# Attention scores on tiles of 32 by 64, an earlier weight fetch and six unused products, in a two-layer attention kernel

## The chip, the cores and the metric

The kernel runs on one core of a Trainium2 chip. A core has five engines that work side by side: TensorE (matrix products, PE in the profile, with PEld for its weight loads), VectorE (DVE), ScalarE (ACT), GpSimd (POOL) and SyncE (SP), which here only issues transfers. The metric is the device time of one execution in microseconds (us); lower is better. Runs of the same kernel are compared by their medians.

## The reference: what is computed

The input is a batch of 8 images of 32 by 32 positions with 512 channels. Two layers follow each other; each adds an attention over its group-normalised input to the input. All numbers are float32.

```python
# layer 0: 16 heads of 32 channels
qkv = gn(x) @ w_qkv
attn = softmax(einsum('bhid,bhjd->bhij', q * 32 ** -0.5, k))
x = x + einsum('bhij,bhjd->bhid', attn, v).reshape(B, N, C) @ w_proj + b_proj
# layer 1: 4 heads of 128 channels, with relative positions
q, k, v = gn(x) @ Wq * 128 ** -0.5, gn(x) @ Wk, gn(x) @ Wv
attn = softmax(q @ k.T + relative_logits(q, pos_emb_w, pos_emb_h))
x = x + (attn @ v) @ Wo
```

N is 1024 positions and C is 512 channels. The group norm gn uses 32 groups of 16 channels per image. The change concerns the scores of layer 0, `q @ k` with a depth of only 32 per head, and the first microseconds of the program.

## The kernel before

The batch is walked one image at a time, and the work of neighbouring images is woven together. While layer 0's attention of image b runs (`attention_0`), the projections, the norms and layer 1's attention of the image before it and the projections of the image after it are issued between its steps. A generator yields after each piece, and `side_by_side` draws pieces of the other work in proportion to a cost. Which instruction stands where on each engine is then decided by the framework's scheduler, which keeps the order of the program only where data demand it.

Each projection (`project_T`, `project_rows`, through `seven`) is a product of 512 by 512 with 1024 positions, done with seven block products in place of eight, on sums and differences of weight quarters and of input quarters. `Matrix.add_up` makes the weight sums: it fetches the weights into a block of SBUF (line 137), makes four differences (L142), and stores them to DRAM (L144), from where the stream of weights (`Stream`) takes them later. `forms` (L328 to L331) makes the sums of the normalised input on VectorE. `by_columns` (the matmul of line 308) cuts each product into four of 32 output columns, tiles of 128 rows by 32 columns of the array.

A step of `attention_0` handles four heads at once, for 128 keys and 512 queries. `front` computes the scores: four products, one for each head, each 32 rows deep and 128 columns wide, into the four banks of one PSUM tile `ps` (L525). ScalarE turns them into exponentials (L533), four banks in one instruction. `back` multiplies the exponentials by v: four products of 128 rows by 32 columns into `acc` (L544), while VectorE adds the exponentials up (L553 and L555). `back` of a step is issued after `front` of the next one. There is one `ps` tile, so a `front` waits until the exponential of the step before has read it. There are 4 x 2 x 8 steps for an image, 512 in all. `finish` divides by the sums (L491 to L513).

The start (`load_first`): eight transfers bring the 1024 rows of the first image, four from SP's queue and four from ScalarE's (L717). TensorE transposes them (L729), ScalarE and VectorE copy the results out (L737, L739), VectorE takes statistics (L244, L245), SP stores the transposed rows away (`put_away`, L213), `group_norm` makes mean and variance (L256 to L281), GpSimd the inverse root (L285), and VectorE normalises in place (L288). Then `forms`, and `before_first`, which projects v, q and k. In the program text v's weights are fetched after `load_first`, from ScalarE's queue, and added up on GpSimd; q's and k's are fetched from SP's queue and added up on VectorE. SP's queue also brings the next image's rows in pieces `xs` (L231).

The fetch, as it was:

```python
        def add_up(self, engine, queue, store, keep=False):
            t = block(f"prep_{self.name}")
...
            queue.dma_start(whole, self.w)
```

Of the kernel before, what the change touches and what calls it, by code (L numbers as in the profile page):

```python
# [9 lines left out]
F32 = mybir.dt.float32  # L10
# [7 lines left out]
P = 128  # L18
# [9 lines left out]
def quick_path(  # L28
# [23 lines left out]
    nc = tc.nc  # L52
# [3 lines left out]
    CC = C // P  # L56
    NT = N // P
    NB = 512
    NH = N // NB
    D0 = 32  # L60
    H1, D1 = 4, 128
    HB = P // D0
# [7 lines left out]
    psum = ctx.enter_context(tc.tile_pool(name="psum", bufs=1, space=PSUM))  # L70
# [4 lines left out]
    def block(name, shape=None, dtype=F32):  # L75
        return mem.tile(shape or [P, CC, N], dtype, tag="block", name=name, bufs=BLOCKS)

    def chunks(block):
        return [block[:, i, :] for i in range(CC)]
# [5 lines left out]
    ident = consts.tile([P, P], F32, tag="ident", name="ident")  # L85
# [34 lines left out]
    def quarter(w, i):  # L120
        k, n = i // 10 - 1, i % 10 - 1
        return w[:, k * HC : (k + 1) * HC, n * HN : (n + 1) * HN]

    class Matrix:
# [4 lines left out]
            self.name = name  # L129
            self.w = w.rearrange("(cc p) n -> p cc n", p=P)[:, :, col0 : col0 + NB]  # L130

        def add_up(self, engine, queue, store, keep=False):

            t = block(f"prep_{self.name}")
            whole = t[:, : CC // 2, :].rearrange("p a (b n) -> p (a b) n", n=NB)
            sums = t[:, CC // 2 :, :].rearrange("p a (b c n) -> p (a b) c n", c=HC, n=HN)
            queue.dma_start(whole, self.w)
            b11, b12, b21, b22 = [quarter(whole, i) for i in (11, 12, 21, 22)]
            for i, (x, y) in enumerate(
                [(b12, b11), (b22, sums[:, 0]), (b22, b12), (b21, sums[:, 1])]  # L140
            ):
                engine.tensor_tensor(sums[:, i], x, y, op=ALU.subtract)  # L142
            d = dram.tile([P, 4, HC, HN], F32, tag="sums", name=f"ws_{self.name}", bufs=8)
            store.dma_start(d, sums)  # L144
            self.t = d
            self.kept = (whole, sums) if keep else None
# [70 lines left out]
    def fetch(kept, x):  # L217
        xT = chunks(x)
        for cc in range(CC):
            nc.sync.dma_start(xT[cc], kept[cc])  # L220
        return xT
# [263 lines left out]
    def normalise(dst, acc_sums, name):  # L485

        su = mem.tile([P, NB], F32, tag="rec", name=f"su_{name}", bufs=2)  # L490
        nc.scalar.copy(su, acc_sums)  # L491
        turned = mem.tile([P, NB], F32, tag="rec", name=f"tu_{name}", bufs=2)
        nc.vector.transpose(turned, su)  # L493
        few = turned.rearrange("p (t c) -> p t c", c=32)[:, :, 0]
        rec = mem.tile([P, NB // 32], F32, tag="few", name=f"rc_{name}", bufs=2)
        nc.vector.reciprocal(rec, few)
        at = check_at[0]
        check_at[0] += 1
        nc.vector.tensor_tensor_reduce(
            out=few,  # L500
            in0=few,
            in1=rec,
            op0=ALU.add,
            op1=ALU.max,
            scale=1.0,
            scalar=0.0,
            accum_out=checks[:, at : at + 1],
        )
        nc.vector.transpose(  # L509
            su.rearrange("p (t c) -> p t c", c=32),  # L510
            rec.unsqueeze(2).to_broadcast([P, NB // 32, 32]),
        )
        nc.gpsimd.tensor_tensor(dst, dst, su, op=ALU.mult)  # L513

    def attention_0(q, k, v, b):

        steps = [(m, h, j) for m in (0, 2, 1, 3) for h in range(NH) for j in range(NT)]
        state = {}

        def front(m, h, j):  # L520
            name = f"0_{b}_{m}_{h}_{j}"
            ps = psum.tile([P, HB, NB], F32, tag="ps", name=f"ps_{name}", bufs=1)
            for r in range(HB):
                rows = slice(r * D0, (r + 1) * D0)
                nc.tensor.matmul(  # L525
                    ps[:, r, :],
                    k[m][rows, j * P : (j + 1) * P],
                    q[m][rows, h * NB : (h + 1) * NB],
                    start=True,
                    stop=True,  # L530
                )
            e = mem.tile([P, HB, NB], F32, tag="e0", name=f"e_{name}", bufs=2)
            nc.scalar.activation(e, ps, AF.Exp, scale=D0 ** -0.5)  # L533
            return e

        def back(m, h, j, e):
            name = f"0_{b}_{m}_{h}_{j}"
            if j == 0:
                state["acc"] = psum.tile([P, NB], F32, tag="acc", name=f"acc_{name}", bufs=1)
                state["first"] = e  # L540
            acc = state["acc"]
            for r in range(HB):
                c0 = (m * HB + r) * D0
                nc.tensor.matmul(  # L544
                    acc[r * D0 : (r + 1) * D0, :],
                    v[:, j, c0 : c0 + D0],
                    e[:, r, :],
                    start=(j == 0),
                    stop=(j == NT - 1),
                )  # L550
            if j == 1:
                state["esum"] = mem.tile([P, HB, NB], F32, tag="es0", name=f"es_{name}", bufs=1)
                nc.vector.tensor_add(state["esum"], state["first"], e)  # L553
            elif j > 1:
                nc.vector.tensor_add(state["esum"], state["esum"], e)  # L555
            if j < NT - 1:
                return
            nc.scalar.copy(q[m][:, h * NB : (h + 1) * NB], acc)
            state["ended"] = (m, h, state["esum"])

        def finish(m, h, esum):
            name = f"0_{b}_{m}_{h}"
            su = psum.tile([P, NB], F32, tag="acc", name=f"sums_{name}", bufs=1)
            for r in range(HB):
                nc.tensor.matmul(  # L565
                    su[r * D0 : (r + 1) * D0, :],
                    ones[:, :D0],
                    esum[:, r, :],
                    start=True,
                    stop=True,  # L570
                )
            normalise(q[m][:, h * NB : (h + 1) * NB], su, name)

        pending = None
        for at in steps:
            if "ended" in state:
                finish(*state.pop("ended"))
            e = front(*at)
            if pending is not None:
                back(*pending)  # L580
            pending = (*at, e)
            yield 2
        back(*pending)
        yield 1
        finish(*state.pop("ended"))
# [126 lines left out]
    def load_first(st):  # L712

        rows = block("x_rows", [P, NT, C])
        for t in range(NT):
            queue = nc.scalar if t % 2 else nc.sync
            queue.dma_start(rows[:, t, :], xf[0, t * P : (t + 1) * P, :])  # L717
        x = block("x0T_0")
        xT = chunks(x)
        for h in range(NH):  # L720
            if h == 0:
                whole = psum.tile([P, CC, NB], F32, tag="ps", name="turned_0", bufs=1)
                banks = [whole[:, cc, :] for cc in range(CC)]
            else:
                banks = [bank(f"turned_1_{cc}") for cc in range(CC - 1)]
                banks.append(psum.tile([P, NB], F32, tag="acc", name="turned_1", bufs=1))
            for t in range(NT // NH):
                for cc in range(CC):
                    nc.tensor.transpose(  # L729
                        banks[cc][:, t * P : (t + 1) * P],  # L730
                        rows[:, h * (NT // NH) + t, cc * P : (cc + 1) * P],
                        ident,
                    )
            for cc in range(CC):
                part = xT[cc][:, h * NB : (h + 1) * NB]
                if h == 0 or cc % 2:
                    nc.scalar.copy(part, banks[cc])  # L737
                else:
                    nc.vector.tensor_copy(part, banks[cc])  # L739
        for cc in (1, 0, 3, 2):  # L740
            statistics(st, xT, cc, "0_0")
        st["kept"] = put_away(xT, "0_0")
        run(group_norm(st, xT, "0_0"))
        st["xn"] = forms(x, "xn0_0")
# [139 lines left out]
    WQ0, WK0, WV0 = [Matrix(w_qkv, i * C, f"qkv{i}") for i in range(3)]  # L884
# [17 lines left out]

    states = [{} for _ in range(B)]
    load_first(states[0])
    WV0.add_up(nc.gpsimd, nc.scalar, nc.gpsimd, keep=True)
    for m in (WQ0, WK0):
        m.add_up(nc.vector, nc.sync, nc.gpsimd, keep=True)
    fill_sel()
    stream = Stream(plan)

    def other_sums():
        for m in (WP, WQ1, WK1, WV1, WO):
            m.add_up(nc.gpsimd, nc.gpsimd, nc.gpsimd)
            yield 0

    def at_once(do):
# [538 lines left out]
```

## Time and profile before

| | |
|---|---|
| median of 6 runs | 3912.12 us (3906.47 to 3914.68) |
| the profiled execution | 3911.84 us |
| its span, first to last instruction | 3910.0 us |
| mean granted TensorE clock | 0.994 |
| TensorE busy | 3817.0 us, 98% |
| VectorE busy | 2519.7 us, 64% |
| ScalarE busy | 1724.6 us, 44% |
| GpSimd busy | 620.8 us, 16% |
| first products of the first projection | from 24.34 us |
| first scores of layer 0 | from 77.7 us |
| last scores of layer 0 | at 3455 us |

In the profile's groups a row gives the line, the engine, the operation, what is written from what, the shape and the number of instructions; then the busy time in us and the mean duration in ns; then the idle time of the engine just before these instructions, and what ended it. For TensorE the shape begins with the tile of the array: 32*128 is 32 rows by 128 columns. The ends of matmuls are modelled, so starts say more than durations. A row of the timeline gives start and duration in us, and merges equal neighbours: "x4" is four instructions. A row of the waits names who waited, for whom, the total in us, the number of times and the longest. PEclk is the share of the full TensorE clock that was granted. A float32 product shows as two weight loads and two matmul records, one for each of its two passes.

### The profile page before, as it was taken

What the parts mean: (1) busy time and instruction counts of PE and PEld (TensorE: products, weight loads), DVE (VectorE), ACT (ScalarE), POOL (GpSimd) and SP (SyncE); (2) the same over time, 40 slices, a digit from 0 to 9 for tenths busy, and PEclk for the clock granted to TensorE, in tenths of its full rate; (3) what the DMA queues carried; (4) which work ended last, traced back from release to release, by engine and by line L of the source; (5) the groups of instructions that cost most, each with busy time, mean ns of one, the idle gap of its engine ahead of it and who ended that gap; (6) DMA issues with size and microseconds to landing.
All of it is one profiled execution on the core that took longest, in us unless ns stands there. A gap on an engine that the chain in (4) does not pass through costs nothing. (4 is left out here: it accounts for less than half of the span.)

```text
span 3910.0 us, 71616 instructions
## 1 busy us (share of the span) xinstructions
PE 3817.0 (98%) x30370; PEld 1416.3 (36%) x30370; DVE 2519.7 (64%) x2905; ACT 1724.6 (44%) x1767; POOL 620.8 (16%) x400
## 2 busy tenths in 40 slices
PE   7999899999999999999999999999999999999998
PEld 4222244232443234432343323433234332344353
DVE  5777675576745867468664686656865568754544
ACT  2554453445434454344544445344453445543132
POOL 1341001121101211012111121111200112011101
PEclk9999999999999999999999999999999999999999
DMA  5221120133202322023120241103311122110401
GB/s 172 75 103 57 34 63 1 39 119 69 58 5 66 103 56 55 12 91 86 42 54 17 91 94 39 44 24 97 88 44 31 31 92 68 32 63 18 124 17 23
DMA packets 482951, 234.19 MB, mean 60 GB/s; under 512 B 269600, under 2 KB 461376, under 8 KB 481600
## 3 DMA queue, kind: packets, MB, share of 16 engines
q1 hardware_dynamic: 470464, 212.69, 20.1%
q0 software_dynamic: 2608, 13.70, 0.9%
q8 instruction: 241, 3.95, 0.4%
q10 hardware_dynamic: 9552, 3.15, 0.4%
q14 instruction: 86, 0.70, 0.1%
HBM read 170.72 MB, written 58.72 MB: 59 GB/s over the span
## 5 line engine op out<-in xcount | busy, mean ns | idle before, releaser
L533 ACT ACTIVATE e<-ps 128x2048 f32<-128x2048 f32 x512 | 961.8, 1879 | 845.8 <-PE ps L525 650.1
L555 DVE TENSOR_TENSOR es<-es,e 128x2048 f32<-128x2048 f32 x384 | 888.1, 2313 | 406.0 <-ACT e L533 403.8
L525 PE MATMUL ps<-q,k 32*128 32x512 f32 x4096 | 591.6, 643 | 33.6 <-ACT e L533 33.5
L643 ACT ACTIVATE e<-ps 128x512 f32<-128x512 f32 x512 | 305.7, 597 | 586.2 <-PE ps L641 549.7
L544 PE MATMUL acc<-e,v 128*32 128x512 f32 x4096 | 549.3, 608 | 0.4 <-ACT su L491 0.4
L640 PE MATMUL ps<-q,k 128*128 128x512 f32 x1024 | 523.6, 593 | 0.3 <-DVE posT L626 0.3
L652 PE MATMUL acc<-e,v 128*128 128x512 f32 x1024 | 521.9, 592 | 0.0
L513 POOL TENSOR_TENSOR q<-q,su 128x512 f32<-128x512 f32 x128 | 214.3, 1674 | 1568.0 <-DVE su L509 1567.3
L663 DVE TENSOR_TENSOR es<-es,e 128x512 f32<-128x512 f32 x384 | 291.8, 760 | 264.5 <-ACT e L643 263.2
L641 PE MATMUL ps<-posT,sel 128*128 128x512 f32 x512 | 406.6, 794 | 0.0
L525 PEld LDWEIGHTS ps<-q,k 32*128 32x128 f32 x4096 | 161.7, 183 | 429.6 <-ACT e L533 213.2
L640 PEld LDWEIGHTS ps<-q,k 128*128 128x128 f32 x1024 | 193.6, 190 | 246.1 <-issue 240.6
L652 PEld LDWEIGHTS acc<-e,v 128*128 128x128 f32 x1024 | 193.1, 189 | 146.7 <-issue 105.0
L544 PEld LDWEIGHTS acc<-e,v 128*32 128x32 f32 x4096 | 81.6, 108 | 387.0 <-issue 342.5
L553 DVE TENSOR_TENSOR es<-e,e 128x2048 f32<-128x2048 f32 x64 | 175.1, 2736 | 38.6 <-ACT e L533 38.6
L493 DVE STREAM_TRANSPOSE tu<-su 128x512 f32<-128x512 f32 x128 | 90.6, 708 | 135.8 <-ACT su L491 135.6
L641 PEld LDWEIGHTS ps<-posT,sel 128*128 128x128 f32 x512 | 97.3, 190 | 122.5 <-issue 122.5
L491 ACT COPY su<-sums 128x512 f32<-128x512 f32 x128 | 74.9, 585 | 149.5 <-PE sums L565 81.3
L661 DVE TENSOR_TENSOR es<-e,e 128x512 f32<-128x512 f32 x64 | 44.2, 691 | 145.7 <-ACT e L643 145.7
L626 DVE TENSOR_TENSOR posT<-pp,posT 32x512 fp32r<-32x512 f32 x128 | 111.9, 874 | 32.0 <-ACT posT L621 30.6
L417 POOL TENSOR_TENSOR k<-b_k,p_k 128x512 f32<-128x512 f32 x32 | 50.3, 1570 | 477.8 <-ACT p_k L382 477.8
L621 ACT CAST posT<-pp 32x512 fp32r<-32x512 f32 x128 | 105.8, 827 | 44.8 <-PE pp L608 43.7
(193 smaller groups left out, 4517.4 us busy)
## 6 DMA issues: line engine op xcount, KB each, us to landing
w_qkv<-ws_qkv SPq DMA_DIRECT2D x168, 128.0 KB, 2.5
d<-x0T SPq DMA_DIRECT2D x32, 512.0 KB, 3.4
x1T<-d SPq DMA_DIRECT2D x32, 512.0 KB, 5.1
d<-x1T SPq DMA_DIRECT2D x32, 512.0 KB, 3.6
x2T<-d SPq DMA_DIRECT2D x32, 512.0 KB, 6.2
w_qkv<-in_L_conv_w_qkv SPq DMA_DIRECT2D x126, 128.0 KB, 2.2
out<-ot SPq DMA_DIRECT2D x240, 64.0 KB, 2.0
xs<-in_x SPq DMA_DIRECT2D x224, 64.0 KB, 2.4
```

What stands on the lines that cost most here:

```text
L513: nc.gpsimd.tensor_tensor(dst, dst, su, op=ALU.mult)
L525: nc.tensor.matmul(ps[:, r, :], k[m][rows, j * P : (j + 1) * P], q[m][rows, h * NB : (h + 1) * NB], start=True, stop=True,)
L533: nc.scalar.activation(e, ps, AF.Exp, scale=D0 ** -0.5)
L544: nc.tensor.matmul(acc[r * D0 : (r + 1) * D0, :], v[:, j, c0 : c0 + D0], e[:, r, :], start=(j == 0), stop=(j == NT - 1),)
L553: nc.vector.tensor_add(state["esum"], state["first"], e)
L555: nc.vector.tensor_add(state["esum"], state["esum"], e)
L626: nc.vector.tensor_sub(rest, logits, greater)
L640: nc.tensor.matmul(ps, k[h][:, keys], q[:, h, queries], start=True, stop=False)
L641: nc.tensor.matmul(ps, sel_flat[:, keys], posT[:, h, queries], start=False, stop=True)
L643: nc.scalar.activation(e, ps, AF.Exp, scale=1.0 / math.sqrt(D1))
L652: nc.tensor.matmul(acc, v[:, j, h * D1 : (h + 1) * D1], e, start=(j == 0), stop=(j == NT - 1),)
L663: nc.vector.tensor_add(state["esum"], state["esum"], e)
```

## The change

Three things change.

1. `front` issues eight score products in a step in place of four: for each half of the 128 keys, one for each head, 32 rows by 64 columns. The halves write the lower and the upper 64 partitions of the same four banks.
2. The fetch of weights is taken out of `add_up` into a method of its own. v's weights are fetched in `load_first`, on SP's queue, right behind the rows of the first image; before, they were fetched after `load_first` on ScalarE's queue. The other weights keep their queue and are fetched right ahead of their sums, as before. The block for v's weights is thereby allotted ahead of that of the transposed rows.
3. After the transposes and the copies of `load_first`, six products of the identity with the first six rows tiles (128 by 128, 512 columns) are issued into a PSUM tile of their own that nobody reads.

```diff
+        def fetch(self, queue):
+            t = self.t = block(f"prep_{self.name}")
+            whole = t[:, : CC // 2, :].rearrange("p a (b n) -> p (a b) n", n=NB)
+            queue.dma_start(whole, self.w)
+
+        def add_up(self, engine, store, keep=False):
+
+            t = self.t
...
-        def add_up(self, engine, queue, store, keep=False):
-
-            t = block(f"prep_{self.name}")
...
-            queue.dma_start(whole, self.w)
...
         def front(m, h, j):
             ps = psum.tile([P, HB, NB], F32, tag="ps", name=f"ps_{name}", bufs=1)
-            for r in range(HB):
-                rows = slice(r * D0, (r + 1) * D0)
-                nc.tensor.matmul(
-                    ps[:, r, :],
-                    k[m][rows, j * P : (j + 1) * P],
-                    q[m][rows, h * NB : (h + 1) * NB],
-                    start=True,
-                    stop=True,
-                )
+            for i in range(2):
+
+                some = slice(64 * i, 64 * i + 64)
+                for r in range(HB):
+                    rows = slice(r * D0, (r + 1) * D0)
+                    nc.tensor.matmul(
+                        ps[some, r, :],
+                        k[m][rows, j * P + 64 * i : j * P + 64 * i + 64],
+                        q[m][rows, h * NB : (h + 1) * NB],
+                        start=True,
+                        stop=True,
+                    )
...
             queue.dma_start(rows[:, t, :], xf[0, t * P : (t + 1) * P, :])
+        WV0.fetch(nc.sync)
         x = block("x0T_0")
...
+        idle = psum.tile([P, CC, NB], F32, tag="ps", name="idle", bufs=1)
+        for t in range(6):
+            nc.tensor.matmul(idle[:, t % CC, :], ident, rows[:, t, :], start=True, stop=True)
         for cc in (1, 0, 3, 2):
             statistics(st, xT, cc, "0_0")
...
-    WV0.add_up(nc.gpsimd, nc.scalar, nc.gpsimd, keep=True)
+    WV0.add_up(nc.gpsimd, nc.gpsimd, keep=True)
     for m in (WQ0, WK0):
-        m.add_up(nc.vector, nc.sync, nc.gpsimd, keep=True)
+        m.fetch(nc.sync)
+        m.add_up(nc.vector, nc.gpsimd, keep=True)
```

More of the change, by code (lines that the diff above doesn't have):

```diff
@@ L912, in other_sums @@
         for m in (WP, WQ1, WK1, WV1, WO):
-            m.add_up(nc.gpsimd, nc.gpsimd, nc.gpsimd)
+            m.fetch(nc.gpsimd)
+            m.add_up(nc.gpsimd, nc.gpsimd)
             yield 0
```

## The prediction

> **What bounds the kernel now.** I read the engine totals first, then the waits of the five middle batches, then the groups, then one score step in the timeline, then the first 31 us.
>
> ```profile
> span 3910.0 us, 71616 instructions
> PE 3817.0 (98%) x30370; PEld 1416.3 (36%) x30370; DVE 2519.7 (64%) x2905; ACT 1724.6 (44%) x1767; POOL 620.8 (16%) x400
> ```
>
> TensorE is busy nearly throughout, the next engine two thirds. Busy matmul time contains fill and drain, so it does not yet say that a nanosecond off TensorE is a nanosecond off the end. The waits from 560 to 3100 us do:
>
> ```profile
> PE y_wo L308 <- DVE a_wo L368: 6.8, 5, 1.4
> PE ps L525 <- ACT e L533: 4.1, 5, 1.1
> PE sums L565 <- ACT q L558: 1.4, 5, 0.3
> ```
>
> That is 12.3 us of waiting in 2540. TensorE's own sequence sets the pace there; over the whole run the scores wait 33.5 us for ScalarE's exponentials, in 28 places near both ends. The groups concerned:
>
> ```profile
> L525 PE MATMUL ps<-q,k 32*128 32x512 f32 x4096 | 591.6, 643 | 33.6 <-ACT e L533 33.5
> L544 PE MATMUL acc<-e,v 128*32 128x512 f32 x4096 | 549.3, 608 | 0.4 <-ACT su L491 0.4
> ```
>
> 4096 records are 512 score steps of four products, each float32 product recorded as two passes. L544 does the same number of 512-column passes in less time, so a score step carries something extra. One step, at 1003.57 to 1005.9 us:
>
> ```profile
> 1003.57 0.40 PE L308 MATMUL z_v<-w_v,x1T 128*32 128x256 f32 x4
> 1003.89 0.71 PE L525 MATMUL ps<-q,k 32*128 32x512 f32 x4
> ...
> 1004.43 0.61 PE L525 MATMUL ps<-q,k 32*128 32x512 f32 x4
> 1004.97 0.64 PE L544 MATMUL acc<-e,v 128*32 128x512 f32 x4
> ```
>
> Read the starts, not the durations. The records' starts (in ns, over all 512 steps, nearly without scatter) give: 429 ns from pass to pass inside one kind of tile; 533 from first to second pass of a score step; 517 from the start of its last product to the first of L544; 453 between L544's two passes; 523 from the last projection product to the score step. Products that run together start 6.7 ns apart. So against 427 ns of streaming, each change of tile form costs 90 to 96 ns, and the first pass after it also shows its weight load: 106 ns for 128 columns, 26 for 32. A step from its first weight load to L544's is 533 + 20 (the fourth product starts 20 ns after the first) + 517 = 1070 ns.
>
> **What the Trainium skill says.** "TensorE: Matmul & The Clock Gate", LDWEIGHTS: a load takes its number of columns divided by 1.2, in ns, whatever the rows: 107 for 128, 53 for 64, 27 for 32. The trace agrees at both ends (106, 26); 64 is not shown. The same page, Part 3, The mechanism: products on different tiles overlap and start about 4 ns apart, matmuls in strict order. Here the spacing is 6.7, and at 99.42 us a product that stands later in the program (z_q, first column tile) starts before three earlier ones (y_q, the other tiles), so the order is not strict across tiles. "TensorEngine Tiling (Array Packing)", Key Properties: changing the tiling mode drains the array; 90 to 96 ns here, and after 128-by-128 tiles it is the same as after 128-by-32, so the columns don't matter. The first page's Part 1 has windows of about 3.4 us after which the clock halves or recovers; here it halves at 14.5 us, 3.6 after the last transpose, and recovers at 28.2.
>
> **The scores, part by part.** Built, the changed kernel has TensorE's order unchanged in all later work; only L525's four products become eight (32 rows by 64 columns, two column halves by four row groups). Per step:
> - Drain before: unchanged, 96, since it belongs to the form that is left. Drain after: unchanged, 90.
> - First-pass load: 64 columns instead of 128. The loads of four row groups run side by side now (106 ns is one load, not four), and so do those of four column tiles in L544 (26 is one of 32 columns, not four). I take it that eight do: 53 exposed, the pass pitch 480. Gain 53. If the halves load one after the other, it stays 106, gain 0.
> - Issue: the eighth product starts 7 × 6.7 = 47 ns after the first, not 20. The drain after a step is counted from its last product (the wait before a step is 523 from the last one, whether 1, 2, 3 or 4 tiles ran before), so this is paid: 27. With the page's 4 ns, an estimate, it would be 16; if the second pass hides it, 0.
> - Streaming: eight 32-by-64 tiles stream the same 2 × 427 ns if all run together. Not shown here; the parts are (four row groups, four column groups).
>
> New step: 480 + 47 + 517 = 1044 against 1070: 26.7 ns less, × 512 = 13.7 us. In the middle nothing covers it, because TensorE waits for nothing. At the ends, where a step waits for the exponential, the chain is step, exponential, step, so the shorter step counts there too. ScalarE and VectorE follow 27 ns earlier per step; with 44% and 64% busy they don't bind.
>
> **The start.** The first projection:
>
> ```profile
> 18.67 2.48 POOL L142 TENSOR_TENSOR prep_qkv<-prep_qkv 128x512 f32<-128x512 f32 x2 [0.87 <-DMA prep_qkv<-in_L_conv_w_qkv]
> 21.24 1.04 POOL L285 TENSOR_TENSOR rstd<-var,neg_half 128x4 f32<-128x4 f32 x1
> 22.27 2.93 POOL L142 TENSOR_TENSOR prep_qkv<-prep_qkv 128x512 f32<-128x512 f32 x2
> ```
> ```profile
> 18.69 1.27 DVE L259 TENSOR_SCALAR avg<-total 128x32 f32<-128x32 f32 x1
> ...
> 20.28 0.89 DVE L281 SCALAR_TENSOR_TENSOR var<-back 128x4 f32<-128x4 f32 x1
> 22.32 4.99 DVE L288 TENSOR_SCALAR x0T<-x0T,back,rstd 128x1024 f32<-128x1024 f32 x4 [1.16 <-POOL rstd L285]
> 27.34 1.23 DVE L328 TENSOR_TENSOR f_xn<-x0T 128x1024 f32<-128x1024 f32 x1
> 28.61 1.22 DVE L329 TENSOR_TENSOR f_xn<-f_xn,x0T 128x1024 f32<-128x1024 f32 x1
> ```
>
> y_v starts at 29.98, when L329 ends, and TensorE then runs nearly full until the first scores at 77.7. So what counts is L329.
> - v's fetch goes from ScalarE's queue (10.9) to SP's behind the rows, where it can issue at 4.38, in the place of the xs loads. Those and SP's later issues move back by about 0.4 us each; nobody needs the xs before 70. Rows and v share the engines at 400 GB/s: rows end near 9, v near 11.3 instead of 18.6.
> - GpSimd's four sums (1.25 each) then run from 11.3 to about 16.5 and leave the norm alone. It slows by their company now: L259 1.27 instead of 0.18, L281 0.89 instead of 0.16, L288 4.99 instead of 2.8 (0.7 each at 394 us). Gain 4.0.
> - The order in the built kernel has a price: q's fetch now stands before the put_away stores, and VectorE's sums of q and k are spread through the norm: six of eight stand before L329, 6 × 0.61 = 3.7 later. The first waits for q's data: 11.3 + 1.3 for three xs (0.2 MB at 150 GB/s) + 2.6 = 15.2, where VectorE arrives at 14.6: 0.6. Queued behind that wait is the whole norm. Bounds 0 to 3.
> - Given back: eight more x_v products done before y_v (four passes of 0.216, 0.9), and a_v, late at 36.84 behind eight sums, no longer late (0.5).
> - The six unused products: 12 passes of 0.43 = 5.1 us from 10.9 to 16, in TensorE's empty time (next work 24.3): nothing, or up to 1 if they ran at half clock. They hold the clock until about 20, not until 24, so I expect it halved again for the first projection. If it held, 8 passes would save 1.7, but y_v waits for L329 anyway: 0 taken, 1.7 at most. The rows' buffer is held 5 us longer; its next user comes after 70.
>
> Sum: −4.0 + 3.7 + 0.6 − 1.4 = −1.1, bounds −4 and +4.
>
> **Sum.** Profiled execution 3911.84 (span 3910.0 and 1.84 around it): −13.7 −1.1 = 3897.0; it lies 0.28 under the median of 3912.12, so 3897.3, given as 3897.
>
> **Rivals.**
> - Issue hidden: the later starts vanish under the first pass. 3912.1 −27.3 −1.1 = 3884. For it: loads do overlap. Against: starts keep their spacing through both passes.
> - Nothing gained: issue is paid in both passes (−53 + 27 + 27), or the start loses what a smaller gain brings. About 3911. Against: today's 20 ns is paid once.
> - Slower: the eight tiles don't run together, at L525's second column half. If its loads wait for the first half's, the pitch stays 533 and only the 27 ns are added: +13.7 −1.1 = 3925. It decides from an exposed load of 80 ns on. The hard form is that the second four products wait until the first four have done both passes, because TensorE does not look far enough ahead: + 853 × 512 = 437 us, 4348. Eight products need 14 later entries set aside, four need 6; only the latter is seen. For both: no 32-by-64 product is in the trace. Against: both directions overlap singly.
>
> **How the numbers follow.** Forecast 0.61, hidden 0.15, nothing gained 0.10, slower by loads 0.09, slower by order 0.05. Forecast and hidden, with the start's bounds, span 3880 to 3902; I carry the range to 3911, so that most of the third case is in and no more than 2 in 10 is out. About 0.2%, 8 us, is what a measurement of this kernel can tell from no change: faster 0.76, within 0.10, slower 0.14.
>
> **What would show it.** L525 as 8192 records of 32*64; pass pitch 480; L544 1044 ns after the step's first load; waits in the middle as small as now. A pitch of 533 shows the serial loads, one near 900 the missing overlap, L544 at 1017 the hidden issue. At the start: y_v near 30, v's sums on GpSimd from 11, the first VectorE sum waiting under 1 us for q, PEclk 0.5 at 24. The forecast is wrong if 64-column loads are not half as long, or if drains depend on columns after all.

## The result, and the profile after

| | before | changed |
|---|---|---|
| median | 3912.48 us (3906.47 to 3915.95, 40 runs) | 3902.11 us (3898.56 to 3907.16, 20 runs) |
| ratio | | 0.9975, 95% interval 0.9969 to 0.9981 |
| the profiled execution, its span | 3911.84 us, 3910.0 us | 3900.62 us, 3898.7 us |
| first score | 77.72 us | 79.26 us |
| first score to the end | 3832.3 us | 3819.5 us |

The change gains 9.8 us by the ratio (7.4 to 12.1). The forecast was 3897; the time is 5 us above it. The page of the changed kernel, answering to the first lines shown of before (busy time, share, instructions):

```profile
span 3898.7 us, 79833 instructions
...
PE 3805.4 (98%) x34478; PEld 1371.1 (35%) x34478; DVE 2516.4 (65%) x2905; ACT 1724.0 (44%) x1767; POOL 622.5 (16%) x400
```

TensorE has 4108 matmuls more, 4096 of them scores and 12 of the unused products, and is busy for 11.6 us less. The groups of the scores and of the products with v:

```profile
L532 PE MATMUL ps<-q,k 32*64 32x512 f32 x8192 | 577.5, 615 | 36.6 <-ACT e L540 36.5
L551 PE MATMUL acc<-e,v 128*32 128x512 f32 x4096 | 547.1, 606 | 0.4 <-ACT su L495 0.4
```

The form is now 32*64 and the count is doubled. One step of the timeline, near the one shown of before:

```profile
994.86 0.39 PE L312 MATMUL z_v<-w_v,x1T 128*32 128x256 f32 x2
995.18 1.11 PE L532 MATMUL ps<-q,k 32*64 32x512 f32 x16
996.22 1.07 PE L551 MATMUL acc<-e,v 128*32 128x512 f32 x8
```

From the scores' first start to that of L551 it is 1.04 us here; before it was 4.97 less 3.89, 1.08. Over all steps the records' starts give 480 ns from the first pass to the second, 47 from a pass's first product to its last, and 517 from the last to L551; from the last product of 512 columns ahead of a step to the step it is 522, as before. The stretch from a step's first product to the next other one, summed over the 64 steps of an image, went from 68.53 to 66.84 us, 26.5 ns a step: 13.5 us in 512 steps.

But from one image to the next the middle went only from 474.5 to 473.2 us (means of five images), 1.3 less where the steps alone give 1.69. What lies beside the steps grew from 406.0 to 406.4 us an image. The waits of TensorE from 560 to 3100 us (total us, times, longest) show where:

```profile
PE y_wo L312 <- DVE a_wo L372: 7.1, 5, 1.4
PE ps L532 <- ACT e L540: 5.2, 5, 1.3
PE sums L572 <- ACT q L565: 1.5, 5, 0.3
```

They were 6.8, 4.1 and 1.4: the three places are the same, and all three have grown, by 1.5 us in five images or 0.3 an image. Where in an image that is, a comparison of ScalarE's exponentials tells: from the 13th of an image to the 21st the time should have fallen by 8 x 26.5 ns, but it was 42.12 us in the kernel before and is 42.19 in the changed one. That is 0.3 of the 0.4 us; the other 0.1 is lost in later steps of the image, where the views list no wait, and stays unexplained. The next lines give the busy time of the engines in that stretch, and for the kernel before also in the 375 us behind it. Before, then changed:

```profile
core 0: us, PE busy (x) PEld busy (x) DVE busy (x) ACT busy (x) POOL busy (x), PEclk, DMA share, GB/s
...
1339.27:1381.39 42.12, 39.98 (x348) 10.67 (x347) 39.60 (x42) 18.22 (x14) 9.09 (x5) 1.00 0.46 84
1381.39:1756.00 374.61, 374.34 (x2952) 148.00 (x2948) 224.94 (x267) 169.75 (x186) 45.25 (x28) 1.00 0.19 52
```
```profile
1335.10:1377.29 42.19, 39.80 (x412) 10.04 (x408) 39.74 (x42) 18.21 (x14) 9.09 (x5) 1.00 0.46 83
```

In the 375 us VectorE is busy for 60% and TensorE waits for nothing. In the 42 us, in which the last projection of one image, the second norm of the next and the exponentials meet, VectorE is busy for 94%, as much as TensorE. Inside the stretch, in the changed kernel:

```profile
1335.10 1.88 ACT L540 ACTIVATE e<-ps 128x2048 f32<-128x2048 f32 x1 [0.44 <-PE ps L532]
1335.89 1.02 POOL L289 TENSOR_TENSOR rstd<-var,neg_half 128x4 f32<-128x4 f32 x1 [1.55 <-DVE var L285]
...
1336.94 2.98 DVE L292 TENSOR_SCALAR x1T<-x1T,back,rstd 128x1024 f32<-128x1024 f32 x4 [1.20 <-POOL rstd L289]
...
1339.84 2.28 DVE L562 TENSOR_TENSOR es<-es,e 128x2048 f32<-128x2048 f32 x1
...
1342.21 1.88 ACT L540 ACTIVATE e<-ps 128x2048 f32<-128x2048 f32 x1 [5.24 <-DVE es L562]
...
1344.15 0.69 PE L532 MATMUL ps<-q,k 32*64 32x512 f32 x8 [0.97 <-ACT e L540]
```

Read it from the bottom: the scores wait for an exponential, that one for a sum on VectorE that is to free a buffer of exponentials, and the sum stands behind the norm's multiplications, which waited for GpSimd's rstd.

The start, first GpSimd, then VectorE:

```profile
13.27 3.72 POOL L146 TENSOR_TENSOR prep_qkv<-prep_qkv 128x512 f32<-128x512 f32 x3 [8.82 <-DMA prep_qkv<-in_L_conv_w_qkv]
...
17.07 1.26 POOL L146 TENSOR_TENSOR prep_qkv<-prep_qkv 128x512 f32<-128x512 f32 x1
```
```profile
17.21 1.67 DVE L146 TENSOR_TENSOR prep_qkv<-prep_qkv 128x512 f32<-128x512 f32 x1 [1.89 <-DMA prep_qkv<-in_L_conv_w_qkv]
...
23.50 0.18 DVE L263 TENSOR_SCALAR avg<-total 128x32 f32<-128x32 f32 x1
...
24.89 0.16 DVE L285 SCALAR_TENSOR_TENSOR var<-back 128x4 f32<-128x4 f32 x1
26.21 2.98 DVE L292 TENSOR_SCALAR x0T<-x0T,back,rstd 128x1024 f32<-128x1024 f32 x4 [1.16 <-POOL rstd L289]
...
31.45 1.21 DVE L333 TENSOR_TENSOR f_xn<-f_xn,x0T 128x1024 f32<-128x1024 f32 x1
```

v's sums end at 18.3 and not at 25.2, and the norm's operations have their short durations: 0.18, 0.16 and 2.98 where they had 1.27, 0.89 and 4.99. But the norm ends no earlier, since six sums for q and k stand in it and the first one waits 1.89 us for its data. Counted from the start of the last transpose of the rows (10.59 us before, 11.44 after; below called "behind the transposes"), y_v starts after 21.37 us (19.39 before), and the first score comes after 67.81 us (67.13 before).

### The profile page after: what moved, and what is told of

Its sections match the earlier page's. It is cut to its first block, busy times and chain, and to the rows that moved or that the text cites. A ratio compares the mean times of both kernels' runs of the same rounds, so it can differ in the third digit from the quotient of the medians.

```text
span 3898.7 us, 79833 instructions
## 1 busy us (share of the span) xinstructions
PE 3805.4 (98%) x34478; PEld 1371.1 (35%) x34478; DVE 2516.4 (65%) x2905; ACT 1724.0 (44%) x1767; POOL 622.5 (16%) x400
## 4 chain that ended last, share of the span: by engine, by line
PE 84%; DVE 9%; ACT 3%; issue 2%; POOL 1%; DMA 1%; SPq 0%; DVEq 0%; POOLq 0%; ACTq 0%
PE ps L647 11%; PE acc L659 11%; PE ps L532 11%; PE acc L551 10%; PE y_k L312 4%; PE y_q L312 4%; PE y_v L312 4%; PE ps L648 3%; PE z_k L312 3%; PE x_v L312 3%; PE x_k L312 3%; PE x_q L312 3%; PE z_v L312 3%; PE z_q L312 2%; ACT e L540 2%; DVE es L562 2%
## 5 line engine op out<-in xcount | busy, mean ns | idle before, releaser
L532 PE MATMUL ps<-q,k 32*64 32x512 f32 x8192 | 577.5, 615 | 36.6 <-ACT e L540 36.5
L551 PE MATMUL acc<-e,v 128*32 128x512 f32 x4096 | 547.1, 606 | 0.4 <-ACT su L495 0.4
L532 PEld LDWEIGHTS ps<-q,k 32*64 32x64 f32 x8192 | 120.4, 130 | 432.6 <-ACT e L540 217.2
L551 PEld LDWEIGHTS acc<-e,v 128*32 128x32 f32 x4096 | 81.5, 108 | 413.6 <-issue 366.0
L633 DVE TENSOR_TENSOR posT<-pp,posT 32x512 fp32r<-32x512 f32 x128 | 111.9, 874 | 31.9 <-ACT posT L628 30.6
```

Of the source, the lines that this page charges most:

```text
L532: nc.tensor.matmul(ps[some, r, :], k[m][rows, j * P + 64 * i : j * P + 64 * i + 64], q[m][rows, h * NB : (h + 1) * NB], start=True, stop=True,
L551: nc.tensor.matmul(acc[r * D0 : (r + 1) * D0, :], v[:, j, c0 : c0 + D0], e[:, r, :], start=(j == 0), stop=(j == NT - 1),)
```

## The experiments

Each was timed beside the kernel before, whose median was 3913.12 us beside e1 to e4, 3911.73 beside e5 to e8 and 3913.91 beside e9 to e12; kernels of different groups are best compared by their ratios.

| kernel | median us | runs | ratio to before, 95% interval |
|---|---|---|---|
| e1, scores alone | 3904.57 | 10 | 0.9976 (0.9967 to 0.9986) |
| e2, early fetch alone | 3913.68 | 13 | 1.0001 (0.9993 to 1.0009) |
| e3, unused products alone | 3910.79 | 13 | 0.9993 (0.9985 to 1.0001) |
| e4, scores on 32 by 32 | 3920.03 | 21 | 1.0020 (1.0013 to 1.0027) |
| e5, changed without unused products | 3901.33 | 7 | 0.9973 (0.9962 to 0.9984) |
| e6, changed, q and k sums after the forms | 3898.39 | 5 | 0.9965 (0.9952 to 0.9979) |
| e7, before, second norm on ScalarE | 3956.60 | 4 | 1.0113 (1.0098 to 1.0129) |
| e8, e1 with the same | 3945.93 | 4 | 1.0093 (1.0078 to 1.0108) |
| e9, before, exponential sum ahead of the norm | 3903.69 | 8 | 0.9972 (0.9961 to 0.9982) |
| e10, e1 with the same | 3890.59 | 5 | 0.9943 (0.9929 to 0.9956) |
| e11, e6 with the same | 3891.22 | 5 | 0.9941 (0.9927 to 0.9954) |
| e12, e11 without unused products | 3889.29 | 5 | 0.9934 (0.9921 to 0.9948) |

### The three parts, each alone (e1, e2, e3)

e1 is the kernel before with the eight products of the diff in `front`. e2 has only the split of the fetch and `WV0.fetch(nc.sync)` behind the rows. e3 has only the six unused products:

```diff
+        idle = psum.tile([P, CC, NB], F32, tag="ps", name="idle", bufs=1)
+        for t in range(6):
+            nc.tensor.matmul(idle[:, t % CC, :], ident, rows[:, t, :], start=True, stop=True)
```

> The kernel before with the eight score products of 32 by 64 alone; the start is as before. Theory A (scores gain in full, the start gives back): a step from its first weight load to the product with v is 480 + 47 + 517 = 1044 ns instead of 1070, times 512 = 13.7 us less, so about 3898.8 us, and the first scores at 77.7 as before. Theory B (part of the scores' gain is lost in waits that grow, and the start is neutral): about 3902, like the whole change.

> The kernel before with the fetch of v's weights behind the first rows and nothing else: four products per score step, no unused products. The order on VectorE becomes that of the changed kernel, with sums of q's and k's weights inside the norm. Theory A: this alone costs 1.6 to 2.7 us, about 3914.5, with the first scores near 79.3 and the first sum on VectorE waiting near 1.9 us for q's weights. Theory B: within 0.5 us of before.

> The kernel before with the six unused products alone. Theory A: they end near 16 us, the clock is halved again before the first projection begins at 24.3, y_v waits for VectorE anyway: within 0.5 us of before, 3912.5. Rival: they hold the clock through the first projection and give 1 to 2 us, about 3911.

e1 took 3904.57, 8.6 us less than the kernel before beside it (3913.12), e2 0.6 more and e3 2.3 less; the sum, 10.3, is about what the whole change gains. Only the first is distinct from zero. By its interval e1 gains 5.5 to 12.9 us, so theory A's 13.7 is just outside and theory B's 10 inside. In e1 the steps have the same starts as in the changed kernel (480, 47, 517), and what lies beside them is again 0.4 us an image longer than before (406.4), while in e2 and e3 it is 406.0. So the growth comes with the scores and not with the start.

In e2 the norm is undisturbed as in the changed kernel, the first sum of q waits 1.54 us, and y_v comes 20.35 us behind the transposes, 1 us later than before; TensorE then does more of x_v ahead of y_v, and the first score, counted from the transposes, is 0.5 us earlier, not later as theory A had it. (Each of these places in the start is read from one profile of a kernel.) In the changed kernel VectorE's chain ahead of y_v ends another 1.3 us later than in e2, and 1.0 of that is the duration of the first sum of q. In e2 this sum began at 16.67 us, just ahead of GpSimd's last sum (16.70), and took 0.69 us, while GpSimd's took 1.80; in the changed kernel GpSimd's last sum began first (17.07, 1.26 us long), and VectorE's, from 17.21, took 1.67. What decided was who came first, by 0.03 and 0.14 us.

In e3 the half clock of the start (PEclk 0.5) lies at 21.0 to 27.8 us instead of 14.5 to 28.2, and the first score comes 1.5 us earlier, counted from the transposes. But the first projection begins at 24.4 us and so has nearly as much half clock as before (3.4 us against 3.9), and TensorE's order in it is another: 57 passes of x_v run ahead of y_v, in the kernel before 34. So the earlier score isn't shown to come from the clock, and the medians don't separate it from nothing.

### Smaller tiles still (e4)

```diff
-            for r in range(HB):
+            for i in range(4):
+                some = slice(32 * i, 32 * i + 32)
...
-                    ps[:, r, :],
-                    k[m][rows, j * P : (j + 1) * P],
+                    ps[some, r, :],
+                    k[m][rows, j * P + 32 * i : j * P + 32 * i + 32],
```

> The kernel before with sixteen score products of 32 by 32 in a step, the start as before. Theory A, a step is 427 + columns / 1.2 + 6.7 x (products - 1) + 517: 427 + 27 + 100 + 517 = 1071 ns, 1 ns more than before, so 3913 us; the pass pitch 454 and the last product 100 ns after the first. Rival (the later starts cost nothing): 427 + 27 + 20 + 517 = 991, 40 us less, 3872. Rival (TensorE cannot look sixteen products ahead): a pitch of some 900 ns and hundreds of us more.

Sixteen tiles are slower than four. The group of its scores:

```profile
L528 PE MATMUL ps<-q,k 32*32 32x512 f32 x16384 | 599.4, 601 | 33.0 <-ACT e L536 32.9
```

The starts give 453 ns from pass to pass, so the exposed load is again that of one tile (453 − 427 = 26). But the last product of a pass starts 116 ns after the first, not 15 x 6.7 = 100: in most steps the first fourteen are 6.7 apart and the last two some 16. This term of theory A was mis-sized. Why the last two are late isn't shown: the second pass's loads are issued between those of the first pass, which is not so with eight products, but that begins with the fifth load already. A step is 453 + 116 + 517 = 1086 ns, 16 more than before, 8.2 us in all; measured are 6.9 by the medians. Of the three sizes tried 64 columns is the best: from 128 to 64 columns the exposed load falls by 53 ns and the train of issues grows by 27; from 64 to 32 the load falls by 27 and the train grows by 69.

### The unused products in company (e5, e12)

e5 is the changed kernel without them; e12 stands further below.

> The changed kernel without its six unused products. If they bring in company what they brought alone (10.79 against 13.12 for before, some 2.3 us), this kernel takes about 3904.5 us, 2.3 above the changed one. If the start is set by the sums on VectorE and the products do nothing there, it takes the changed kernel's time within 1 us (3901 to 3903); the one profile of each that there is (y_v 20.35 us behind the transposes without the products, 21.37 with them) even says 1 us less, 3901. The first score is expected 66 to 67 us behind the last transpose of the rows.

3901.33 against 3902.11: they bring nothing that can be measured there, nor in e12 against e11. The pair shows why. In the changed kernel and in e5 y_v comes 21.37 us behind the transposes (so the 20.35 of e2 was not for want of the products) and the first score 67.81 and 67.80, not 66 to 67. The half clock lasts from 20.6 to 30.9 us with the products and from 13.5 to 30.6 without them. What they take away of it is time in which TensorE has no other work; the first projection, from about 27 us on, has 3.8 and 3.7 us of half clock in the two.

### The start without sums in the norm (e6)

```diff
+        forms_done[0] = nc.vector.tensor_sub(s4, a12, s2)
...
         m.fetch(nc.sync)
-        m.add_up(nc.vector, nc.gpsimd, keep=True)
+        with tc.issue_after(forms_done[0].ins):
+            m.add_up(nc.vector, nc.gpsimd, keep=True)
```

> The changed kernel, with the eight VectorE sums for q's and k's weights held until the forms of the first batch are done. Theory: the early fetch of v's weights freed the norm of GpSimd (some 4 us), and the six q and k sums that moved into the norm, with 1.9 us of waiting for q's weights, took it back; then y_v starts 15.5 to 16.5 us behind the last transpose (before 19.4, changed 21.4), the first score comes 62 to 63.5 us behind it (changed 67.8), and the time falls by 4 to 5 us, to 3897 to 3898. Rival: the order of the start doesn't reach the total, because TensorE then waits for q's sums or for the clock instead; then y_v comes early and the first score doesn't, and the time stays within 1.5 us of the changed kernel's 3902.

VectorE in the start of e6:

```profile
19.32 0.16 DVE L285 SCALAR_TENSOR_TENSOR var<-back 128x4 f32<-128x4 f32 x1
20.64 2.98 DVE L292 TENSOR_SCALAR x0T<-x0T,back,rstd 128x1024 f32<-128x1024 f32 x4 [1.17 <-POOL rstd L289]
...
24.92 1.22 DVE L334 TENSOR_TENSOR f_xn<-f_xn,x0T 128x1024 f32<-128x1024 f32 x1
...
28.33 4.90 DVE L146 TENSOR_TENSOR prep_qkv<-prep_qkv 128x512 f32<-128x512 f32 x8
```

The variance is there at 19.3 instead of 24.9, y_v starts 16.50 us behind the transposes, 4.9 earlier than in the changed kernel, and the first score 62.52 behind them, 5.3 earlier. In the profile the end follows (span 3892.8, 5.9 less): from the first score on e6 takes 3819.6 us and the changed kernel 3819.5, with as much half clock (27.4 and 27.9 us). The median falls by 3.7 us; by the ratios the difference is 0.9965 against 0.9975, with intervals that overlap. What the early fetch gives and what the sums take back is shown in the start, and in these two profiles it reaches the end; by the medians that is likely, not settled.

### Work off VectorE, the wrong way (e7, e8)

```diff
+        if name[0] == "1":
+            shift = small.tile([P, CC], F32, tag="shift", name=f"shift_{name}")
+            nc.gpsimd.tensor_tensor(shift, mean, rstd, op=ALU.mult)
+            nc.gpsimd.tensor_scalar(shift, shift, -1.0, None, op0=ALU.mult)
+            for cc in range(CC):
+                nc.scalar.activation(
+                    xT[cc],
+                    xT[cc],
+                    AF.Identity,
+                    bias=shift[:, cc : cc + 1],
+                    scale=rstd[:, cc : cc + 1],
+                )
...
+            return
```

> The kernel before, with the second norm's four multiplications of 1024 elements (0.73 us each) on ScalarE instead of VectorE, as scale and bias of one activation each, and two small operations on GpSimd for the bias. It is the base for the next kernel. Theory: the waits of TensorE for y_wo and ps (10.9 us of the 12.3 in the middle) stand at a stretch in which VectorE is the bound, so taking 2.9 us an image off it shortens them by a half or more: part beside the score steps 405 us an image against 406.0, time 3904 to 3908. Rival: ScalarE, which gets 4 us of work there, becomes the bound and its exponentials come later; then the waits for ps grow and the time is 3913 or above.

> The kernel that has the 32 by 64 scores alone, with the second norm's four multiplications on ScalarE, like the one ahead of it. Theory: the 0.34 us an image that the shorter scores give back are VectorE's stretch at the second norm, which didn't get shorter; with that stretch relieved the part beside the score steps is the same in this kernel and in the one ahead of it (within 0.1 us an image), and the gain between the two is the whole 13.5 us (12.5 to 14.5), time 3891 to 3894. Rival: the 0.34 us come from somewhere else, TensorE's own spacing or the rest of the products; then this kernel's part is again 0.3 us an image above that of the one ahead, and the gain is 9 to 11 us.

Both are more than 40 us slower than the kernel that each was made from. TensorE's waits of e7 from 560 to 3100 us, and ScalarE in the stretch:

```profile
PE ps L540 <- ACT e L548: 28.2, 5, 5.7
```
```profile
1351.97 1.24 ACT L292 ACTIVATE x1T<-x1T,shift,rstd 128x1024 f32<-128x1024 f32 x1 [8.38 <-POOL shift L290]
1353.12 1.86 ACT L548 ACTIVATE e<-ps 128x2048 f32<-128x2048 f32 x1
...
1355.34 3.51 ACT L292 ACTIVATE x1T<-x1T,shift,rstd 128x1024 f32<-128x1024 f32 x3
```

ScalarE stood for 8.38 us at the first multiplication, which waited for shift, with an exponential queued behind it whose scores were done at about 1346 us; the other three (1.2 us each) stand ahead of the next one. So not its load but its order hurts: an instruction that waits holds up one that could run. One wait of 5.7 us in each image is also enough for a half clock of 6.8 us, which none of these places had before. The question of this pair is not answered by it: e8's part beside the steps is 411.3 to 412.5 us an image, e7's 411.4 to 411.8.

### The sum of exponentials ahead of the norm (e9, e10)

The edit orders VectorE alone; the order on the other engines stays the same.

```diff
-                nc.vector.tensor_add(state["esum"], state["esum"], e)
+                added[0] = nc.vector.tensor_add(state["esum"], state["esum"], e)
...
+            hold = name[0] == "1" and added[0] is not None
+            with tc.issue_after(added[0].ins) if hold else nullcontext():
+                nc.vector.tensor_scalar(
...
```

> The kernel before, with one edit in VectorE's order: the four multiplications of the second norm stand behind the next sum of exponentials instead of ahead of it (two behind that one, two behind a later one). TensorE's, ScalarE's and GpSimd's orders are unchanged. Theory: in the norm VectorE waits 1.2 us for rstd and then works 3 us on the multiplications, while a sum of 2.28 us whose input is ready stands behind them; that sum holds one of the two buffers of exponentials, so ScalarE and then TensorE wait. With the sum ahead the waits for y_wo and ps (10.9 us in five images) go, the part beside the score steps falls from 406.0 to about 403.9 us an image, and the time by 7 times 2.2, to 3896 to 3899. Rival: the waits stay or move to another sum, because VectorE has as much work in the stretch as before; then the time is within 4 us of 3912.

> The scores on tiles of 32 by 64 alone, with VectorE's sum of exponentials ahead of the second norm's multiplications. Theory: what the shorter scores give back (0.34 us an image) is given back at that one place, where VectorE's chain has its own length; without it the part beside the score steps is the same as in the kernel ahead of this one within 0.1 us an image, and the gain of the scores is the whole 13.5 us (12 to 15), time 3883 to 3886. Rival: it is given back anywhere VectorE or ScalarE sets the pace; then this kernel's part is again 0.3 us above and the gain is 10 us or less, time 3887 to 3890.

VectorE in e9, and TensorE's longest waits in the middle, e9 and then e10:

```profile
1334.76 2.28 DVE L558 TENSOR_TENSOR es<-es,e 128x2048 f32<-128x2048 f32 x1
1336.96 0.69 DVE L435 TENSOR_TENSOR x2T<-p_wo,x2T 128x512 f32<-128x512 f32 x1
1337.96 1.53 DVE L290 TENSOR_SCALAR x1T<-x1T,back,rstd 128x1024 f32<-128x1024 f32 x2 [0.31 <-POOL rstd L285]
```
```profile
PE y_wo L311 <- DVE a_wo L371: 5.5, 5, 1.1
```
```profile
PE y_wo L311 <- DVE a_wo L371: 6.8, 5, 1.4
```

The sum now fills the time in which rstd is made; VectorE waits 0.31 us for it instead of 1.20, and the scores' wait for ScalarE (4.1 us) is gone from the list. The part beside the steps falls by 1.1 us an image, to 404.9, half of the 2.2 that I expected, since the wait for a_wo stays, and the median, 3903.7, lies between the two forecasts. The stretch of 42.12 us is now 41.04, and VectorE is busy for 96% of it:

```profile
1334.33:1375.37 41.04, 39.91 (x348) 10.67 (x348) 39.52 (x42) 18.36 (x14) 10.87 (x5) 1.00 0.46 86
```

And with the short scores, in e10, the part beside the steps is 405.2 us, 0.35 more than in e9; the waits for a_wo make 0.26 of it (6.8 less 5.5 us in five images). So the theory that the gain is given back at the norm's stall falls, and the rival holds: take that stall away, and the same amount is given back at the next place where TensorE waits for VectorE. In e10 VectorE runs without a listed gap from 1333.5 us until the a_wo for which TensorE waits is done at 1346.6, so what sets the pace is VectorE's work in the stretch, not the one operation. The times alone don't decide: e10 is 13.1 us below e9 by the medians, which would fit the theory, and 11 by the ratios, and the intervals are wider than the 2 us in question.

### Both edits together (e11, e12)

> The changed kernel with both edits: the q and k sums behind the first forms, and the sum of exponentials ahead of the second norm's multiplications. The two lie at different ends of the run and should add: the kernel ahead of this one less the gain of the start (e6 against e1: first score 73.2 against 79.3 us, median 3898.4 against 3904.6), so 3877 to 3880. If the start's gain is given back later, 3883 to 3886.

> The kernel ahead of this one without the six unused products. In the changed kernel they made no difference that could be seen (3901.3 without them, 3902.1 with them), but there TensorE waited for VectorE. Here y_v comes some 5 us earlier, when the clock without them is still at half. If they are worth something at all it is the half clock between about 22 and 31 us, 2 to 4 us, so 3880 to 3884. If not, within 1.5 us of the kernel ahead of this one.

Both forecasts for e11 missed: the gains at the start and in the middle didn't add up in the medians. e10, e11 and e12 lie within 2 us of each other, 11 to 13 below the changed kernel, and all three beat both kernels. In e11's profile the first score comes 64.83 us behind the transposes (e6: 62.52), because 9.0 us of its first projection ran at half clock and 3.9 of e6's. From the first score on e11 takes 1.5 us more than e10, with 28.6 us at half clock against 24.1, so that its end lies only 0.4 us ahead of e10's. e12 came 1.9 us below e11, outside both its forecasts, but the intervals overlap widely; its first projection has 8.3 us of half clock, so here too the products had hardly changed that. Whether e6's edit is worth its 4 us on top of e9's stays open.

## Why the prediction was right, and where it fell short

- **The score step** ("480 + 47 + 517 = 1044 against 1070") was right to the nanosecond: the load of 64 columns is exposed for 53, eight tiles overlap, and the issue of the later products is paid once. The load time for 64 columns that the Trainium skill's "TensorE: Matmul & The Clock Gate", LDWEIGHTS, gives and the trace of before couldn't show is now measured: 480 − 427 = 53 ns. The 427 comes out of the runs too. From pass to pass of a step it is 533, 480 and 453 ns for 128, 64 and 32 columns; these differ by 53 and 27, so a column costs 0.83 ns, and 427 is left for none. The rivals at this place (issue hidden, serial loads, tiles that don't overlap) are all ruled out by these starts. e4 shows that 6.7 ns an issue doesn't hold for any number of tiles.
- **"In the middle nothing covers it, because TensorE waits for nothing"** is the step that fell short. It is true for nine tenths of an image. In the other 42 us VectorE sets the pace, and what TensorE saves there turns into waiting; with the 0.1 us lost in later steps it is 0.4 us an image, 2.0 in the five middle ones, of the 13.7. The lines that say so stood in the prediction: 6.8 us for a_wo and 4.1 for ps. I read their sum, small against 2540, instead of asking why there was any wait at all in those places; and of the 28 waits "near both ends" five are those of the middle. "With 44% and 64% busy they don't bind" is the same error: in an image from the middle of the kernel before, VectorE is busy for 81% of the first 58 us, for 94% of the next 42 and for 60% of the rest.
- **The start** was forecast at −1.1 and is about +0.7 by the first score, counted from the transposes. The seven profiles that have the start of before (before, e1, e4, e7 to e10) lie between 66.82 and 67.13 us, the two with that of the changed kernel (changed, e5) at 67.8. Right were the undisturbed norm (0.18, 0.16, 2.98), the six sums in it, and nearly the 1.4 us given back between y_v and the first score (47.7 to 46.4). Mis-sized were the arrival of v's weights (GpSimd begins at 13.3, not at 11.3, and ends at 18.3, not at 16.5) and the wait for q's weights, 0.6 in the sum, 1.89 in the profile and inside its bounds; and the first of the six sums took 1.67 us instead of 0.61, beside GpSimd's last one (17.07 to 18.33). That last microsecond was a matter of chance: in e2 the two began in the other order.
- **The unused products** were credited with nothing, and nothing can be measured. That they hold the clock until about 20 us, too short for the first projection, was right (half from 20.6 to 30.9).
- **The sum.** −13.5 for the steps and +2.0 given back make −11.5 from the first score on; the profiles have −12.8. The 1.3 between is less than the clock alone can make, since from the first score on the two executions spent 34.9 and 27.9 us at half clock. With +1.5 for the later first score the profiles come to −11.2, and the runs to −9.8. The forecast, −14.8 by its two terms, lacked the give-back (2.0) and had the start 1.8 too low; −11.0 is left, within the interval of 7.4 to 12.1.

## What to carry to other kernels

A wait that is small in the sum marks a place where another engine sets the pace, and a gain made elsewhere is given back there; look at the busy shares in a window around each such wait before counting a gain in full. Ahead of an instruction that waits, look at what is queued behind it: putting the sum of exponentials ahead of the norm's multiplications, in VectorE's order alone, was worth as much as the whole change, and the same pattern on ScalarE cost 44 us. An edit that moves a transfer earlier also moves what depends on it, here into the one chain that it was to relieve.

## What the runs showed of the hardware

- The clock makes single profiles a poor scale for a few microseconds: the executions profiled here, apart from e7 and e8, had between 34 and 51 us at half clock, in pieces of 3.4 us and multiples of it, and two executions of nearly the same program don't have them in all the same places.
- One TensorE wait of 5.7 us in each image brought a half clock of 6.8 us (e7), which began 4.0 us into the wait; waits of 1.1 to 1.4 us brought none.
- VectorE's sums and tensor-scalar operations that began beside a running GpSimd sum of 128 by 512 ended only after it: a VectorE sum of the same size took 1.67 us in the changed kernel and 1.75 in e5 instead of 0.61, ending 0.55 us after GpSimd's in both, and short operations in before took 0.9 to 1.3 us instead of 0.16 to 0.18. A transpose in before (0.24 us) and batch statistics in e2 (0.6 us each) ran beside it in their usual time. In e2, where VectorE's sum began first, GpSimd's was the one that got longer (1.80 us instead of 1.26).
- With sixteen 32-by-32 tiles in a pass the issues of the last two slow down from 6.7 to some 16 ns.
